# Attention steps moved between slots, routing spread over the tiles, and the first expert's weight splits placed later

## The chip, the core and the metric

The kernel runs on one core of a Trainium2 chip. A core has a matrix engine (TensorE, "PE"), a vector engine (VectorE, "DVE"), a scalar engine (ScalarE, "ACT"), GpSimd ("POOL") and SyncE ("SP"), which here only issues DMAs. Every engine takes its own instructions strictly in order and waits on semaphores for the others. The metric is the device time of one execution in microseconds (us).

## What is computed

4096 tokens of width 256 pass through three residual stages:

```python
x = x + 0.5 * ffn(layernorm(x))     # stage 1
x = x + attn(layernorm(x))          # attention in groups of 64 tokens, 16 heads of 16
x = x + 0.5 * ffn(layernorm(x))     # stage 2, the same weights
# ffn(x): shared = silu(x @ sg) * (x @ su) @ sd                  (256 -> 2048 -> 256)
#   routed: RMS norm, 8 router logits, top 2 of 8 experts, weights from a softmax;
#   each expert takes its first 640 tokens: silu(x @ rg[e]) * (x @ ru[e]) @ rd[e]   (256 -> 1024 -> 256)
# attn: q, k get an RMS norm times ln_w; causal softmax inside each group of 64 tokens
```

## The kernel before

Every fp32 product is made of three fp16 products: both operands are split into a high and a low half, and high x high, high x low, low x high are summed in PSUM (`TERMS`, L35).

The program has four phases. **Phase a**: front of stage 1 (layernorm, router, scatter) and the shared FFN of blocks 0 to 3 (a block is 512 tokens, four tiles of 128). **Phase b**: stage 1's eight experts. **Phase c**: the shared FFN of blocks 4 to 7 of stage 1 and then of blocks 0 to 6 of stage 2, with the attention of 32 tiles woven in. **Phase d**: stage 2's eight experts and the last shared block.

A shared block has 16 chunks (L406). A chunk is `gate_up` (L350): six matmuls of 512 columns into a gate bank and six into an up bank, out of three banks that rotate. In phase c ACT takes the tanh of the gate bank (L367), DVE multiplies it with the bank (`sl`, L368) and with the up bank (`sl`, L373), ACT casts the result to fp16 (`hh`, L375), and DVE takes the rest (`hl`, L376, two inputs in SBUF). The down product, twelve matmuls of 256 columns (L384), is held back until the next chunk's `gate_up` has been issued (`defer`, L97); its third matmul is the first that reads `hl`.

Attention and routing of a tile are a generator (`tile2`, L839) whose `yield`s are steps. `Tiles` (L730) starts a tile every `GAP_C` = 4 slots and takes one step of each live tile per slot; `drive` (L779) gives one slot per chunk. A tile's steps are: layernorm (`stats`, `two`), a transpose by DMA (`xt`), q, k, v (`pqk`, `pv`, L584 to L598), q and k norms and fp16 halves (`ss`, `qk`, `QK`, L602 to L620), transposes by DMA (`QT`, L624), scores (`psc`, `S`, L628 to L637), softmax (`amx`, `S` minus the maximum on POOL at L641, exp, `e16`, on POOL at L652), a transpose (`ET`, L655), the product with the values (`py`, `Y`), a transpose (`yt`, L681), projection (`pao`, `y`), and the front of stage 2 (`front_steps`, L697). POOL also forms `yp`, `X` and `xa` (all L172), the powers of -0.5 (L150, L592), parts of the routing weights (L245 to L266), and it issues the scatters: per tile four small copies (L339) and two indirect DMAs (L341).

The fourth tile of each block runs `route` (L239): the top two of eight for four tiles at once (L250 to L255), softmax weights on POOL, positions by small matmuls, then `scatters` (L310), one tile per step, tied behind an anchor instruction of POOL (L313).

In the experts (L466) each chunk's weights are loaded by SP, split by ACT (L105) and DVE (L106) into fp16 halves, and used; the chunk's buffers are two deep.

The order on each engine is not that of the source: a scheduler orders the instructions when the program is built. `issue_after` forces an instruction behind a named one on the same engine.

Of the kernel before, what the change touches and what calls it, by code (L numbers as in the profile page):

```python
# [20 lines left out]
P = 128  # L21
H = 256
# [3 lines left out]
WS = 16.0  # L26
XP = UP * WS
NB = 8
BT = 512
E = 8  # L30
# [7 lines left out]
class Net:  # L38
# [160 lines left out]
    @contextmanager  # L199
    def behind(self, on=True, *engines):  # L200

        with ExitStack() as st:
            if on:
                for k in engines:
                    st.enter_context(self.tc.issue_after(self.latest[k]))
            yield
# [18 lines left out]
    def logits(self, fb, t, xt):  # L225
# [11 lines left out]
        nc.scalar.copy(fb["L"][:, t], p)  # L237

    def route(self, R, b, fb, tiles):  # L239

        nc = self.nc
        sm = self.sm
        mv, rstd = fb["mv"], fb["rstd"]
        rs = sm.tile([P, 4], F32, name="rs")
# [3 lines left out]
        nc.gpsimd.tensor_tensor(out=rs, in0=rs, in1=self.mhalf[:, :4], op=ALU.pow)  # L248
        L = sm.tile([P, 4, E], F32, name="Ls")
        nc.vector.tensor_tensor(out=L, in0=fb["L"][:, :, 0], in1=fb["L"][:, :, 1], op=ALU.add)  # L250
        mx = sm.tile([P, 4, E], F32, name="mx")
        ix = sm.tile([P, 4, E], U32, name="ix")
        for t in range(4):
            nc.vector.max(out=mx[:, t, :], in_=L[:, t, :])
            nc.vector.max_index(out=ix[:, t, :], in_max=mx[:, t, :], in_values=L[:, t, :])  # L255
        dl = sm.tile([P, 4], F32, name="dl")
        nc.vector.tensor_tensor(out=dl, in0=mx[:, :, 1], in1=mx[:, :, 0], op=ALU.subtract)
        nc.gpsimd.tensor_tensor(out=dl, in0=dl, in1=rs, op=ALU.mult)
        nc.gpsimd.tensor_scalar_mul(dl, dl, 1.0 / WS)
        nc.gpsimd.tensor_tensor(out=dl, in0=self.e1, in1=dl, op=ALU.pow)  # L260
        w1 = sm.tile([P, 4], F32, name="w1")
        nc.gpsimd.tensor_scalar_add(w1, dl, 1.0)
        nc.gpsimd.tensor_tensor(out=w1, in0=w1, in1=self.mone, op=ALU.pow)
        nc.gpsimd.tensor_scalar_mul(w1, w1, 0.5 / WS)
        nc.gpsimd.tensor_tensor(out=dl, in0=dl, in1=w1, op=ALU.mult)
        nc.gpsimd.tensor_tensor(out=w1, in0=w1, in1=dl, op=ALU.subtract)  # L266
        ef = sm.tile([P, 4, 2], F32, name="ef")
        nc.vector.tensor_copy(ef, ix[:, :, 0:2])
        yield
        oh = sm.tile([P, 4, 2, E], F32, name="oh")  # L270
# [4 lines left out]
        nc.vector.tensor_tensor(out=M, in0=oh[:, :, 0, :], in1=oh[:, :, 1, :], op=ALU.add)  # L275
        yield
        pp = self.m1([P, 4, E], F32, "pp")
        nc.tensor.matmul(pp, lhsT=self.tri, rhs=M, start=True, stop=False)
# [11 lines left out]
        nc.vector.tensor_reduce(out=pos, in_=pk, axis=AX.X, op=ALU.add)  # L290
        yield
        df = sm.tile([P, 4, 2], F32, name="df")
        nc.vector.scalar_tensor_tensor(
# [10 lines left out]
        last = self.scatters(R, b, fb, di, w1, dl, ef, 1 if b == NB - 1 else tiles.apart)  # L304
        if b == NB - 1 or tiles.apart == 1:
            yield from last
        else:
            tiles.extra.append(last)

    def scatters(self, R, b, fb, di, w1, dl, ef, every):  # L310

        for t in range(4):
            with self.tc.issue_after(self.anchor.ins):  # L313
                self.scatter(R, b, fb, t, di, w1, dl, ef)
            for _ in range(every):
                yield
# [149 lines left out]
    def experts(self, R, rg, ru, rd, cur, also=iter(())):  # L466

        nc = self.nc
        for e in range(E):
            x, ids, wts = cur["x"], cur["id"], cur["w"]  # L470
# [3 lines left out]
            for c in range(8):  # L474
                if e == 0 and c < 2:
                    wc, wd = self.chunks[c]
                else:
                    r = self.raw.tile([P, 2, 2, P], F32, name="re", tag="raw")
                    for i, s in enumerate((rg, ru)):
                        nc.sync.dma_start(  # L480
                            out=r[:, i], in_=s[e, :, c * P:(c + 1) * P].rearrange("(k p) f -> p k f", p=P))
                    r2 = self.raw.tile([P, H], F32, name="re2", tag="raw2")
                    nc.sync.dma_start(out=r2, in_=rd[e, c * P:(c + 1) * P])
                    wc = self.raw.tile([P, 2, 2, 2, P], F16, name="wc")
                    self.split(wc[:, 0], wc[:, 1], r)
# [55 lines left out]
    def attn_init(self, ln_w):  # L541
# [15 lines left out]
        for i in range(2):  # L557
# [3 lines left out]
            self.V2.append(v)  # L561

    def attn_tile(self, R, j, x2, new_fb):

        nc = self.nc
# [33 lines left out]
        yield  # L599
        yield  # L600
# [5 lines left out]
        for i in range(2):  # L606
# [8 lines left out]
            else:  # L615
# [4 lines left out]
                    out=s[:, :, 1::2, :], in0=src, in1=s[:, :, 0::2, :], op=ALU.subtract)  # L620
        yield
        QT = a.tile([P, 2, 24, 64], F16, name="QT")
        for g in range(2):
            nc.sync.dma_start_transpose(  # L624
                out=QT[:, g], in_=self.QK[g * 64:(g + 1) * 64].rearrange("p j c -> p (j c)"))
        yield
        yield
        S = a.tile([P, 16, 64], F32, name="S")  # L628
        for g in range(2):
            p = self.m1([P, 8, 64], F32, "psc")  # L630
            for jj in range(8):
                nc.tensor.matmul(
                    p[:, jj, :], lhsT=QT[:, g, 2 * jj:2 * jj + 2, :].rearrange("p r q -> p (r q)"),
                    rhs=QT[:, g, 16 + jj, :], start=True, stop=True)
            nc.vector.tensor_tensor(  # L635
                out=S[:, g * 8:(g + 1) * 8, :], in0=p,
                in1=self.mask.unsqueeze(1).to_broadcast([P, 8, 64]), op=ALU.add)  # L637
        yield
        mx = self.sm.tile([P, 16], F32, name="amx")
        nc.vector.tensor_reduce(out=mx, in_=S, axis=AX.X, op=ALU.max)  # L640
        self.anchor = nc.gpsimd.tensor_tensor(  # L641
            out=S, in0=S, in1=mx.unsqueeze(2).to_broadcast([P, 16, 64]), op=ALU.subtract)
        for g in range(2):
            for d in range(2):
                nc.scalar.copy(  # L645
                    V2[d * 64:(d + 1) * 64, g, :, :, 0:32],
                    vs[g * 64:(g + 1) * 64].rearrange("p l (j c) -> p l j c", c=32))
        yield
# [5 lines left out]
        ET = a.tile([P, 16, P], F16, name="ET")  # L654
        nc.sync.dma_start_transpose(out=ET, in_=e16.rearrange("p h l k -> p (h l k)"))  # L655
        yield
        yield
        Y = a.tile([P, 2, 8, 16], F32, name="Y", tag="yy")
        for g in range(2):
# [7 lines left out]
            for r in range(2):  # L667
# [3 lines left out]
                    in1=rc[sl].unsqueeze(2).to_broadcast([64, 8, 16]), op=ALU.mult)  # L671
        yield
        y = self.tok.tile([P, H], F32, name="y")
# [6 lines left out]
        for r in range(2):  # L680
            nc.sync.dma_start_transpose(out=yt[:, r], in_=yp[r * 64:(r + 1) * 64])  # L681
        yield
        yield
# [115 lines left out]
def macaron(ctx, tc, x, w_qkv, ln_w, w_proj, router_w, rg, ru, rd, sg, su, sd, out):  # L799
# [20 lines left out]

    def tail(R, h, b, t):
        if t == 3:
            yield from n.route(R, b, fbs[(h, b)], tiles)
# [101 lines left out]
```

## Time and profile before

| what | value |
|---|---|
| median of 3 runs (lowest, highest) | 1809.57 us (1809.15, 1809.93) |
| profiled execution, device time | 1811.83 us |
| its span | 1809.8 us |
| busy PE, DVE, ACT, POOL | 1777.4, 1194.7, 949.8, 752.2 us |
| matmuls | 13652 |
| granted TensorE clock, mean | 0.999 |

The profiled execution took 2.3 us more than the median of the timed ones, and 2.0 us of it lie outside the span. A busy PE counts every matmul from its start to its modelled end, and the ends overlap the next starts, so stalls shorter than about 0.16 us don't show as idle time.

### The profile page before, as it was taken

The numbers are of one execution on the slowest core, as the hardware profiler recorded it, in microseconds if no ns is written. First come the engines' busy times: TensorE is split into PE (matmuls) and PEld (weight loads), VectorE is DVE, ScalarE is ACT, GpSimd is POOL, SyncE is SP. The second block draws the span as 40 slices with busy tenths as digits, with TensorE's granted clock in tenths as the row PEclk, the third lists the DMA queues.
The fourth block names the chain that finished last, engine by engine and source line by source line (L and its number), as shares of the span: only waits on it lengthen the run. The fifth ranks groups of instructions, "written<-read, shape, count | busy, mean of one in ns | idle before, by whom it ended". The sixth has DMA issues, their size and how long they took to land.

```text
span 1809.8 us, 37358 instructions
## 1 busy us (share of the span) xinstructions
PE 1777.4 (98%) x13652; PEld 1200.8 (66%) x13652; DVE 1194.7 (66%) x2905; ACT 949.8 (52%) x2053; POOL 752.2 (42%) x1072
## 2 busy tenths in 40 slices
PE   9999999999999999999999999999999999999998
PEld 5666657777777556665666666566555677777765
DVE  7766636666665678877777778778655566666643
ACT  5433334555554456666666666656333355555542
POOL 3676711211112445576767777675430011122210
PEclk9999999999999999999999999999999999999999
DMA  7333133555543356767677675756212045455420
GB/s 222 105 102 116 38 69 88 120 118 120 115 112 66 70 101 101 133 119 138 125 130 144 114 147 108 143 100 125 56 22 71 18 109 115 111 119 121 100 47 13
DMA packets 437545, 185.16 MB, mean 102 GB/s; under 512 B 302193, under 2 KB 434733, under 8 KB 437360
## 3 DMA queue, kind: packets, MB, share of 16 engines
q1 hardware_dynamic: 418880, 160.81, 40.7%
q0 software_dynamic: 17664, 21.17, 6.9%
q8 instruction: 107, 1.75, 0.4%
q10 hardware_dynamic: 816, 0.79, 0.1%
q14 instruction: 78, 0.64, 0.1%
HBM read 78.16 MB, written 42.21 MB: 67 GB/s over the span
## 4 chain that ended last, share of the span: by engine, by line
PE 65%; DVE 9%; issue 9%; POOL 8%; ACT 5%; DMA 2%; SPq 1%; POOLq 0%; DVEq 0%; ACTq 0%
PE pgu L360 42%; PE po L384 21%; POOL xg L341 2%; DVE sl L368 2%; DVE hl L376 2%; POOL S L641 1%; DVE amx L640 1%; DVE S L635 1%; DVE sl L373 1%; ACT sl L367 1%; POOL e L652 1%; ACT V L645 1%; POOL X L339 1%; POOL ss L592 1%; DMA y<-acc 1%
## 5 line engine op out<-in xcount | busy, mean ns | idle before, releaser
L360 PE MATMUL pgu<-xb,sgu 128*128 128x512 f16 x3072 | 736.1, 379 | 10.3 <-DVE sl L368 5.6
L375 ACT CAST hh<-sl 128x512 f16<-128x512 f32 (+2 forms) x512 | 272.9, 533 | 538.1 <-DVE sl L373 513.2
L360 PE MATMUL pgu<-xe,wc 128*128 128x384 f16 (+1 forms) x3072 | 497.6, 299 | 0.0
L360 PEld LDWEIGHTS <-sgu 128*128 128x128 f16 x3072 | 292.8, 98 | 282.8 <-issue 15.2
L373 DVE SCALAR_TENSOR_TENSOR sl<-pgu,sl 128x512 f32<-128x512 f32 (+2 forms) x512 | 301.1, 588 | 265.0 <-PE pgu L360 230.8
L376 DVE TENSOR_TENSOR hl<-sl,hh 128x512 f16<-128x512 f32 (+2 forms) x512 | 316.4, 618 | 152.4 <-ACT hh L375 139.3
L384 PEld LDWEIGHTS <-hh 128*128 128x128 f16 x3328 | 321.3, 98 | 106.8 <-ACT hh L375 3.9
L360 PEld LDWEIGHTS <-wc 128*128 128x128 f16 x3072 | 300.6, 98 | 91.8
L384 PE MATMUL po<-sdw,hh 128*128 128x256 f16 x2048 | 349.7, 272 | 2.5 <-ACT hh L375 2.2
L384 PE MATMUL po<-sdw,hl 128*128 128x256 f16 x1024 | 249.1, 273 | 10.0 <-DVE hl L376 9.8
L384 PE MATMUL po<-wd,hh 128*128 128x256 f16 x1280 | 222.5, 273 | 0.0
L506 POOL DMA_INDIRECT out_dram<-eo,eidscatter x40 | 64.3, 1607 | 342.4 <-DVE eo L505 308.7
L371 ACT ACTIVATE sl<-pgu 128x384 f32<-128x384 f32 (+1 forms) x336 | 159.0, 473 | 75.7 <-PE pgu L360 48.5
L384 PEld LDWEIGHTS <-hl 128*128 128x128 f16 x1664 | 162.7, 98 | 51.3 <-DVE hl L376 16.8
L506 POOL DMA_INDIRECT acc<-eo,eidscatter x40 | 64.9, 1621 | 293.4 <-DVE eo L505 259.4
L368 DVE SCALAR_TENSOR_TENSOR sl<-sl,pgu 128x512 f32<-128x512 f32 x176 | 120.1, 682 | 54.9 <-ACT sl L367 52.3
L341 POOL DMA_INDIRECT xg<-X,di x128 | 133.4, 1042 | 45.6 <-issue 23.0
L384 PE MATMUL po<-wd,hl 128*128 128x256 f16 x640 | 148.2, 273 | 0.0
L367 ACT ACTIVATE sl<-pgu 128x512 f32<-128x512 f32 x176 | 104.3, 593 | 29.2 <-PE pgu L360 28.2
L105 ACT ACTIVATE wc<-re 128x512 f16<-128x512 f32 x124 | 78.1, 630 | 73.4 <-PE pgu L360 59.3
L106 DVE SCALAR_TENSOR_TENSOR wc<-re,wc 128x512 f16<-128x512 f32 x124 | 85.6, 690 | 25.0 <-ACT wc L105 19.1
L641 POOL TENSOR_TENSOR S<-S,amx 128x1024 f32<-128x1024 f32 x32 | 63.6, 1988 | 70.4 <-DVE amx L640 70.0
(159 smaller groups left out, 1730.7 us busy)
## 6 DMA issues: line engine op xcount, KB each, us to landing
re<-in_L_ffn_rg_dram SPq DMA_DIRECT2D x124, 128.0 KB
re<-in_L_ffn_ru_dram SPq DMA_DIRECT2D x124, 128.0 KB
re<-in_L_ffn_rd_dram SPq DMA_DIRECT2D x124, 128.0 KB
y<-acc SPq DMA_DIRECT2D x64, 128.0 KB
y<-in_L_attn_x_dram SPq DMA_DIRECT2D x32, 128.0 KB
acc<-xr SPq DMA_DIRECT2D x16, 256.0 KB
out_dram<-xr SPq DMA_DIRECT2D x16, 256.0 KB
x<-y SPq DMA_DIRECT2D x28, 128.0 KB
```

What stands on the lines that cost most here:

```text
L106: nc.vector.scalar_tensor_tensor(out=lo, in0=src, scalar=WS, in1=hi, op0=ALU.mult, op1=ALU.subtract)
L341: i = nc.gpsimd.indirect_dma_start(out=R["xg"][:, :], out_offset=bass.IndirectOffsetOnAxis(ap=di[:, t, k:k + 1], axis=0), in_=X, in_offset ...
L360: nc.tensor.matmul(p, lhsT=wc[:, w, i, k, :], rhs=x[:, 2 * a + k, :], start=(j == 0), stop=(j == 5))
L367: nc.scalar.activation(s, p, AF.Tanh, scale=0.5 / XP)
L368: nc.vector.scalar_tensor_tensor(out=s, in0=s, scalar=1.0, in1=p, op0=ALU.add, op1=ALU.mult)
L371: self.latest[0] = nc.scalar.activation(s, p, AF.Silu, scale=1.0 / XP).ins
L373: self.latest[1] = nc.vector.scalar_tensor_tensor(out=s, in0=ps[1], scalar=1.0 / XP / (2.0 * XP if tanh else 1.0), in1=s, op0=ALU.mult, op ...
L375: nc.scalar.copy(h[0], s)
L376: nc.vector.tensor_tensor(out=h[1], in0=s, in1=h[0], op=ALU.subtract)
L384: nc.tensor.matmul(o, lhsT=h[a][:, t * P:(t + 1) * P], rhs=wd[:, w], start=(c == 0 and j == 0 and t % 2 == 0), stop=(c == nch - 1 and j == 2),
L506: i = nc.gpsimd.indirect_dma_start(out=R["acc"][:, :], out_offset=bass.IndirectOffsetOnAxis(ap=ids[:, t:t + 1], axis=0), in_=eo, in_offset ...
L641: self.anchor = nc.gpsimd.tensor_tensor(out=S, in0=S, in1=mx.unsqueeze(2).to_broadcast([P, 16, 64]), op=ALU.subtract)
```

## The change

Line numbers of the changed file are not used below; the operations keep the names and lines of the kernel before.

1. **Attention's steps.** One `yield` fewer between q, k, v and the q/k norms; one more before `QT`, one more after it (three slots from the `QT` transposes to the scores instead of two), one more after `ET`, none between `Y` and `yp`, one more after `yt`. The copies of the values into `V2` (L645), four in one step, become two in the scores' step and two in the next. `vs` has two buffers. The tiles' slot counter starts at -2.
2. **Routing.** The top two of eight are found tile by tile (`top2`). `route` is cut at other places: the POOL chain for `rs` first, the exponential and its companions two steps later, `w1` and what follows one step after that.
3. **Scatters.** In phase c one tile is scattered every four slots, after three empty slots, as an extra generator; before, the four tiles of a block were scattered in four successive slots. The pool of `X` has 8 buffers instead of 6. Two more POOL powers (L150 in `front_steps`, L592) become anchors for scatters.
4. **Experts.** The splits of expert 0's chunks 2 to 7 are forced, on ACT and DVE, behind the last silu and `sl` of the chunk two before.

```diff
+    def top2(self, fb, t):
+        nc = self.nc
+        if t == 0:
+            fb["mx"] = self.sm.tile([P, 4, E], F32, name="mx")
+            fb["ix"] = self.sm.tile([P, 4, E], U32, name="ix")
+        L = self.sm.tile([P, E], F32, name="Ls")
+        nc.vector.tensor_tensor(out=L, in0=fb["L"][:, t, 0], in1=fb["L"][:, t, 1], op=ALU.add)
+        nc.vector.max(out=fb["mx"][:, t, :], in_=L)
+        nc.vector.max_index(out=fb["ix"][:, t, :], in_max=fb["mx"][:, t, :], in_values=L)
...
     def scatters(self, R, b, fb, di, w1, dl, ef, every):
+        for _ in range(3 if every == 4 else 0):
+            yield
         for t in range(4):
...
+        marks = []
...
-                    self.split(wc[:, 0], wc[:, 1], r)
                     wd = self.raw.tile([P, 2, H], F16, name="wd")
-                    self.split(wd[:, 0], wd[:, 1], r2)
+                    with self.behind(e == 0, 0, 1, mark=marks[-2]):
+                        self.split(wc[:, 0], wc[:, 1], r)
+                        self.split(wd[:, 0], wd[:, 1], r2)
...
+                marks.append(list(self.latest))
...
+    def values(self, V2, vs, g):
+        for d in range(2):
+            self.nc.scalar.copy(
+                V2[d * 64:(d + 1) * 64, g, :, :, 0:32],
+                vs[g * 64:(g + 1) * 64].rearrange("p l (j c) -> p l j c", c=32))
...
-        nc.gpsimd.tensor_tensor(out=ss, in0=ss, in1=self.mhalf[:, :2], op=ALU.pow)
+        self.anchor = nc.gpsimd.tensor_tensor(out=ss, in0=ss, in1=self.mhalf[:, :2], op=ALU.pow)
...
-        vs = a.tile([P, 2, H], F16, name="vs")
+        vs = a.tile([P, 2, H], F16, name="vs", bufs=2)
...
         yield
-        yield
         for i in range(2):
...
         yield
+        yield
         QT = a.tile([P, 2, 24, 64], F16, name="QT")
...
+        yield
         yield
         yield
         S = a.tile([P, 16, 64], F32, name="S")
...
-        self.stats(y, fb["mv"][:, t, :], fb["rstd"][:, t:t + 1], keep is None)
+        self.stats(y, fb["mv"][:, t, :], fb["rstd"][:, t:t + 1], True)
...
-    with n.phase("c", BT, 2, 6, SLC):
+    with n.phase("c", BT, 2, 8, SLC):
         n.attn_init(ln_w)
-        tiles = Tiles(tile2, 32, GAP_C, 1)
+        tiles = Tiles(tile2, 32, GAP_C, GAP_C)
+        tiles.slot = -2
```

The order in which the changed program's instructions stand was compared with the order before. PE has the same 13652 matmuls. In phase c the order before differs from tile to tile: one tile in four carries the scatters, one the top two of eight, two others the POOL chains. In the changed order the four tiles of a block are nearly alike. On POOL a tile reads

```
S (L641), X, xa (L172), 4 copies (L339), 2 scatters (L341), e (L652), yp (L172), ss (L592), QK (L613 x2, L619), rstd, arstd (L150)
```

from the 9th or 10th tile to the 29th, with the `rs` chain at the end of one tile in four and the chain for `dl` and `w1` ahead of `rstd` in the next. On DVE four chunks of a tile read

```
mv amv ve ve S S hl nm nm amx sl368 sl373 | sl368 hl sl373 | rc rc Y hl ss sl368 qk qk vs Ls sl373 | mx ix hl sl368 y st st sl373
```

On ACT the four copies into `V2` still stand together in most tiles, behind exp and `e`, and ahead of a chunk's `hh`.

More of the change, by code (lines that the diff above doesn't have):

```diff
@@ L199, in behind @@
     @contextmanager
-    def behind(self, on=True, *engines):
+    def behind(self, on=True, *engines, mark=None):
         with ExitStack() as st:
@@ L204, in behind @@
                 for k in engines:
-                    st.enter_context(self.tc.issue_after(self.latest[k]))
+                    st.enter_context(self.tc.issue_after((mark or self.latest)[k]))
             yield
@@ L242, in route @@
         sm = self.sm
-        mv, rstd = fb["mv"], fb["rstd"]
+        mv, rstd, mx, ix = fb["mv"], fb["rstd"], fb["mx"], fb["ix"]
         rs = sm.tile([P, 4], F32, name="rs")
@@ L248, in route @@
         nc.gpsimd.tensor_tensor(out=rs, in0=rs, in1=self.mhalf[:, :4], op=ALU.pow)
[L249 to L255, printed above, removed]
+        yield
         dl = sm.tile([P, 4], F32, name="dl")
         nc.vector.tensor_tensor(out=dl, in0=mx[:, :, 1], in1=mx[:, :, 0], op=ALU.subtract)
[L258 to L266, printed above, removed]
         ef = sm.tile([P, 4, 2], F32, name="ef")
         nc.vector.tensor_copy(ef, ix[:, :, 0:2])
-        yield
         oh = sm.tile([P, 4, 2, E], F32, name="oh")
@@ L276, in route @@
         yield
+        nc.gpsimd.tensor_tensor(out=dl, in0=dl, in1=rs, op=ALU.mult)
+        nc.gpsimd.tensor_scalar_mul(dl, dl, 1.0 / WS)
+        nc.gpsimd.tensor_tensor(out=dl, in0=self.e1, in1=dl, op=ALU.pow)
         pp = self.m1([P, 4, E], F32, "pp")
@@ L291, in route @@
         yield
+        w1 = sm.tile([P, 4], F32, name="w1")
+        nc.gpsimd.tensor_scalar_add(w1, dl, 1.0)
+        nc.gpsimd.tensor_tensor(out=w1, in0=w1, in1=self.mone, op=ALU.pow)
+        nc.gpsimd.tensor_scalar_mul(w1, w1, 0.5 / WS)
+        nc.gpsimd.tensor_tensor(out=dl, in0=dl, in1=w1, op=ALU.mult)
+        nc.gpsimd.tensor_tensor(out=w1, in0=w1, in1=dl, op=ALU.subtract)
         df = sm.tile([P, 4, 2], F32, name="df")
@@ L304, in route @@
         last = self.scatters(R, b, fb, di, w1, dl, ef, 1 if b == NB - 1 else tiles.apart)
-        if b == NB - 1 or tiles.apart == 1:
+        if b == NB - 1:
             yield from last
@@ L598, in attn_tile @@
             out=vs[:, 1, :], in0=pv, scalar=1.0 / XP, in1=vs[:, 0, :], op0=ALU.mult, op1=ALU.subtract)
-        yield
         yield
@@ L625, in attn_tile @@
                 out=QT[:, g], in_=self.QK[g * 64:(g + 1) * 64].rearrange("p j c -> p (j c)"))
+        yield
         yield
@@ L637, in attn_tile @@
                 in1=self.mask.unsqueeze(1).to_broadcast([P, 8, 64]), op=ALU.add)
+        self.values(V2, vs, 0)
         yield
@@ L642, in attn_tile @@
             out=S, in0=S, in1=mx.unsqueeze(2).to_broadcast([P, 16, 64]), op=ALU.subtract)
[L643 to L647, printed above, removed]
+        self.values(V2, vs, 1)
         yield
@@ L655, in attn_tile @@
         nc.sync.dma_start_transpose(out=ET, in_=e16.rearrange("p h l k -> p (h l k)"))
+        yield
         yield
@@ L671, in attn_tile @@
                     in1=rc[sl].unsqueeze(2).to_broadcast([64, 8, 16]), op=ALU.mult)
-        yield
         y = self.tok.tile([P, H], F32, name="y")
@@ L681, in attn_tile @@
             nc.sync.dma_start_transpose(out=yt[:, r], in_=yp[r * 64:(r + 1) * 64])
+        yield
         yield
@@ L821, in tail @@
     def tail(R, h, b, t):
+        n.top2(fbs[(h, b)], t)
         if t == 3:
```

## The prediction

> **What bounds the kernel now.** I read the page first, then PE's waits in the stretch where attention is woven in, then busy times by stage, then single instructions.
>
> ```profile
> PE 1777.4 (98%) x13652; PEld 1200.8 (66%) x13652; DVE 1194.7 (66%) x2905; ACT 949.8 (52%) x2053; POOL 752.2 (42%) x1072
> ```
>
> The waits of PE from 720 to 1280 us (total, times, longest):
>
> ```profile
> PE po L384 <- DVE hl L376: 8.5, 13, 0.7
> PE pgu L360 <- DVE sl L368: 5.2, 6, 0.9
> ```
>
> Busy times by stage (window, length, then busy us and count of PE, PEld, DVE, ACT, POOL, the granted clock, DMA share, GB/s):
>
> ```profile
> 800.00:1240.00 440.00, 426.49 (x3606) 268.75 (x3603) 338.44 (x871) 283.83 (x600) 312.07 (x429) 1.00 0.68 130
> 1240.00:1300.00 60.00, 57.85 (x475) 36.30 (x473) 41.72 (x107) 27.49 (x55) 34.64 (x55) 0.97 0.33 61
> 1300.00:1345.00 45.00, 45.00 (x293) 27.36 (x291) 28.57 (x70) 14.90 (x27) 13.06 (x34) 1.00 0.12 33
> ```
>
> PE is the bound at the full clock, so only its stalls can be won. In attention's stretch its waits are for DVE. Idle time understates them: taken from the starts of successive matmuls, against 0.216 us for 512 columns and 0.109 for 256, PE loses 18.1 us in 800 to 1240, 5.7 in 587 to 800, 4.5 in 1240 to 1300, nothing in 1300 to 1345. Attention's stage thus holds 28 us, the two entries into the experts another 4.6; the rest of the span next to nothing.
>
> ```profile
> 969.57 1.93 POOL S L641
> ...
> 1051.05 1.93 POOL S L641
> ```
>
> In the chain of waits (start, us, what) the pattern returns every 81.5 us, a block of four tiles: 20.4 per tile. Pure PE work of a tile's four chunks is 19.6 (four times 2.59 + 1.31, from the chain's runs of twelve matmuls, and 4.0 of attention). So 0.8 per tile is stalled.
>
> **Part 4, the experts' splits.** On ACT before:
>
> ```profile
> 251.08 0.63 ACT L105 ACTIVATE wc<-re 128x512 f16<-128x512 f32 x1 [6.65 <-DMA re<-in_L_ffn_rg_dram]
> 251.62 0.60 ACT L375 CAST hh<-sl 128x512 f16<-128x512 f32 x1
> ...
> 252.28 0.61 PE L384 MATMUL po<-sdw,hh 128*128 128x256 f16 x4 [1.66 <-ACT hh L375]
> ```
>
> A split that waits for its weights stands ahead of the shared block's `hh`, and PE waits. At 1363 it is the same (idle 1.73 and 0.24). From start to start the losses are 2.2 and 2.4. Afterwards the splits stand behind chunk 0's silu; two chunks of some 5 us each remain until chunk 2 needs them, and a split takes 1.0 on ACT and 1.1 on DVE. I count 4.3 gained.
>
> **Parts 1 to 3, a gain first.** Following the new order, DVE no longer has a tile with the top two, the exponent, the residual and the scores together; every local stall of before has slack on PE's side. If no queue were longer than PE's 19.6, nearly all 28 us would go.
>
> **The cost.** Two scatters and four copies now stand in every tile of POOL, between `S` and `e`, and `ss`, without which DVE cannot do `qk`, stands behind them. This closes a loop through DVE and POOL, which I add up by differences of starts:
> - DVE, from a tile's last `sl` (L373) to `amx`: four small ones 0.3, `S` twice 1.2, `hl` 0.6, `nm` twice 0.25, `amx` 1.21, less 0.08 of overlap: 3.5 (starts of 512-column instructions in a row lie 0.60 apart though each takes 0.68).
> - POOL: hop 0.13, `S` 1.90, `X` and `xa` 1.24, copies and scatters 3.0 (row pair below: 966.46 to 969.57 is 3.1), `e` 2.13, `yp` 0.62, `ss` 0.7: 9.7.
> - DVE: `qk` twice and `vs` 1.15, `Ls` 0.1, `sl` 0.68, ACT's `hh` with hops 0.73, `hl` 0.6, `sl` 0.6, `y` 0.33, `st` 0.66, `sl` 0.68: 5.6 with the first hop.
>
> Sum 18.8, below 19.6: no stall.
>
> ```profile
> 966.46 0.17 POOL L339 COPY X<-tokid 128x1 f32<-128x1 f32 x1
> ...
> 967.14 1.01 POOL L341 DMA_INDIRECT xg<-X,di  x1 [0.16 <-POOL X L339]
> 968.46 1.09 POOL L341 DMA_INDIRECT xg<-X,di  x1 [0.30 <-issue]
> 969.57 1.92 POOL L641 TENSOR_TENSOR S<-S,amx 128x1024 f32<-128x1024 f32 x1
> ...
> 687.17 2.13 POOL L652 TENSOR_TENSOR e<-S,e 128x1024 f16<-128x1024 f32 x1 [2.24 <-ACT e L651]
> ...
> 687.65 2.20 DVE L376 TENSOR_TENSOR hl<-sl,hh 128x512 f16<-128x512 f32 x1 [1.40 <-ACT hh L375]
> ```
>
> The last two rows change this. `hl` usually takes 0.69; here it takes 2.20, ending 0.55 after `e`. The Trainium skill (SBUF — State Buffer, "Who interferes with whom") says that a DVE instruction with two SBUF inputs and a GpSimd instruction that reads SBUF exclude each other for their whole length, whichever starts first. Row and rule agree that it blocks; the rule adds that it must happen at every overlap and in both directions. It speaks against this change, because three of the loop's `hl` now fall on long POOL work: one becomes ready 0.1 before POOL's `S` ends (costs POOL 0.43), one while `e` runs, since its `hh` stands on ACT behind exp, `e16` and four `V2` copies (0.50), one while the last `QK` runs (0.64). Counted from the end of `amx`: POOL's `S` runs to 2.0, and `sl368`, `sl373`, `hh` make the first `hl` ready at 1.9; `e` runs from 6.75 to 8.9, while exp (to 3.15), `e16` (4.2), the copies (6.6) and `hh` (7.2) make the second ready at 7.3; with the delays `ss` ends at 10.65, the last `QK` runs from 12.95 to 14.1, and the third is ready at 13.35. With the rule the loop is 20.3, without it 18.8. I take 20.3: the second and third overlaps hold by 0.4 or more, and in place of the first `hl` would meet `X`.
>
> So each of the 21 tiles with scatters costs 20.3 - 19.6 = 0.7, together 15. Two POOL chains lie in the loop too: `rs` (about 2.3) ends some 0.85 after `amx`, the chain of `dl` and `w1` (4.3) delays `rstd` by about 0.4, and `M`, `n` cost DVE 0.25: 1.5 per block, five times 7.5. Less 2 of slack before the loop first binds: 21 us of stalls, where those tiles had 18.5. These are worked out from rows; their ends are 0 (locks missed) and 34 (0.6 more per tile).
>
> **The rest.** Tiles 0 to 8 have no scatters, so a loop of under 19.6: I take 3.5 of stalls for 5.7. The gap at 1285 to 1294, 4.4 us with the clock at half for 3.4, stood beside six scatters in a row that are now spread; whether they cause it the trace can't say. I count half, 2. Three more small DVE instructions per tile (0.15 each) run while `hl` waits for `hh`. The `V2` copies and the second `vs` cost no work; PE's cover for them is that chunk's 1.8 us before `hl` is needed. The extra slots lengthen a tile by some six slots: the last routing stands about 19 chunks before the end of phase c, instead of 23, and 4 scatter slots fit. SP's queue keeps its ten issues per tile (some 12 us of 19.6); `QT` gets a slot more, so it lands earlier than needed. Eight `X` buffers cover the 23 slots that an `X` lives.
>
> Sum: -4.3 + 2.5 - 2.2 - 2 = -6 us. The profiled execution's span of 1809.8 would become 1804. I take off the same from the median, 1809.6 to 1803.6; the 2.3 between profiled and timed stays out.
>
> **Rivals.**
> - *The locks are missed*, the loop is 18.8 and PE bound: 21 us of stalls shrink to 2, so 1785. For it: a regular order, and in before most `hl` took 0.69. Against: the starts above.
> - *The loop is longer still (slower).* If `hl` goes ahead of `e` and the scatters take what they did from 953.24 to 956.93, 3.7 instead of 3.1, POOL's chain grows by 0.6 in 21 tiles: +13, so 1816. It ends slower than before once the loop passes 20.6, beyond the tie by 0.2% from about 20.8.
> - *A wait for a DMA takes over*, as `ET`, `yt` and `QT` share SP with the store of `y`: 0.5 per tile over 32 tiles is +16, so 1820. Against: each landing has over a slot to spare.
> - That the steps don't move is excluded by the order of the built program.
>
> **Chances.** The forecast 0.50, spread 1797 to 1811; locks missed 0.17; longer loop 0.27; DMA 0.06. A measurement of this kernel tells about 0.2%, 3.6 us. Faster: 0.33 of the forecast's and all of the second, 0.50. Slower: nearly all of the last two and a little of the first, 0.34. The rest 0.16. The range leaves out half of the fast case and the ends of the slow ones.
>
> **What would show it.** Right: waits of PE for `hl` twice per tile, evenly, period 20.4 to 20.7 per tile; `hl` of 1.3 to 2.2 us beside `e` and `QK`; no wait for `hh` at either entry into the experts. Wrong: periods of 19.6 and no waits (locks missed), or POOL's `S` more than 21 us apart; or PE waiting for a transpose.

## The result and the profile after

The changed kernel takes **1815.78 us** (median of 7 runs, 1815.11 to 1816.61), the one before 1809.36 us beside it (7 runs, 1808.24 to 1811.58). The ratio is **1.0034** (95% interval 1.0023 to 1.0044): slower by some 6 us. The profiled execution took 1816.61 us, its span 1814.8, so 5.0 more than the span before.

The page's line of busy times:

```profile
PE 1781.6 (98%) x13652; PEld 1197.6 (66%) x13652; DVE 1265.6 (70%) x2953; ACT 955.1 (53%) x2053; POOL 768.6 (42%) x1072
```

DVE is busy 71 us longer than before. It has 48 instructions more, but most of this isn't work: an instruction that is held while one of POOL's runs counts as busy. From 800 to 1240 us the `hl` alone are lengthened by 49 us in all, against 6 before. PE's waits from 720 to 1280 us (total, times, longest):

```profile
PE po L389 <- DVE hl L381: 16.5, 36, 0.8
PE pl L230 <- DMA xb<-X: 0.5, 1, 0.5
```

The waits for `sl` are gone, those for `hl` have doubled. (L381 is L376 of the kernel before; from here on lines are those of the changed file: `sl` L373 and L378, `hh` L380, `S` on POOL L658, `e` L665, `ss` L607, copies and scatters L344 and L346.) Busy times by stage, columns as in the prediction:

```profile
800.00:1240.00 440.00, 423.65 (x3527) 260.48 (x3526) 392.54 (x878) 281.49 (x595) 312.98 (x418) 1.00 0.64 127
1240.00:1300.00 60.00, 57.47 (x498) 36.34 (x497) 49.53 (x111) 32.74 (x65) 37.52 (x49) 1.00 0.51 92
```

In attention's stage DVE is busy 392.5 us in place of 338.4, and in the same 440 us PE gets through fewer matmuls (3527 against 3606). In the prediction's own measure, starts of successive matmuls less 0.216 or 0.109 us each, PE's lost time by stretch is:

| stretch, us | what is there | before | after | difference | forecast |
|---|---|---|---|---|---|
| 205-275 and 1345-1400 | entries into the experts | 5.16 | 0.00 | -5.2 | -4.3 |
| 587-800 | entry into attention, tiles 0 to 8 | 5.63 | 8.58 | +3.0 | -2.2 |
| 800-1240 | tiles 9 to 29 | 18.01 | 25.75 | +7.7 | +2.5 |
| 1240-1300 | last tiles, scatters | 4.52 | 3.26 | -1.3 | -2 |
| elsewhere | start, phases a and b, the end | 7.1 | 7.8 | +0.7 | 0 |
| sum | all | 40.4 | 45.4 | +5.0 | -6 |

A stall of 0.55 us that ends at 587.45 before and at 585.42 after is counted under "elsewhere" in both. But for rounding, the sum of the differences is the difference of the spans, so nothing is missing. The splits and the last tiles came out near the forecast; the two terms of attention's phase did not.

Now one tile of the steady state, in the timeline of POOL (start, length, instruction, in brackets the idle time before it and what ended it):

```profile
1044.20 1.90 POOL L658 TENSOR_TENSOR S<-S,amx 128x1024 f32<-128x1024 f32 x1 [1.54 <-DVE amx L657]
1046.06 0.68 POOL L172 TENSOR_TENSOR X<-z,X 128x256 f16<-128x256 f32 x1
1046.69 0.68 POOL L172 TENSOR_TENSOR xa<-z,xa 128x256 f16<-128x256 f32 x1
1047.31 0.65 POOL L344 COPY X<-tokid 128x1 f32<-128x1 f32 x1
...
1050.01 0.98 POOL L346 DMA_INDIRECT xg<-X,di  x1 [0.31 <-issue]
1051.01 2.14 POOL L665 TENSOR_TENSOR e<-S,e 128x1024 f16<-128x1024 f32 x1
1053.09 1.14 POOL L172 TENSOR_TENSOR yp<-Y,yp 128x256 f16<-128x256 f32 x1
1054.34 0.73 POOL L607 TENSOR_TENSOR ss<-ss,mhalf 128x2 f32<-128x2 f32 x1
...
1064.92 1.90 POOL L658 TENSOR_TENSOR S<-S,amx 128x1024 f32<-128x1024 f32 x1 [2.14 <-DVE amx L657]
```

and what DVE does meanwhile:

```profile
1046.90 1.01 DVE L381 TENSOR_TENSOR hl<-sl,hh 128x512 f16<-128x512 f32 x1
...
1050.50 3.21 DVE L381 TENSOR_TENSOR hl<-sl,hh 128x512 f16<-128x512 f32 x1
...
1058.08 0.98 DVE L381 TENSOR_TENSOR hl<-sl,hh 128x512 f16<-128x512 f32 x1 [0.34 <-ACT hh L380]
...
1063.57 1.21 DVE L657 TENSOR_REDUCE amx<-S 128x16 f32<-128x1024 f32 x1
```

From `S` to `S` 20.72 us pass, where the prediction's loop has 20.3. From `S` to the end of `ss` POOL waits for nothing but its own issue (twice 0.3); from there DVE is at work, with small gaps, until `amx`. `hl` without company takes 0.68; here it takes 1.01, 3.21 and 0.98, and the first small copy on POOL 0.65 where the others take 0.17. These are the locks, two or three per tile, near where they were forecast. The row of 3.21 occurs in one tile of four; in the others `hl` begins some 0.4 after `e` and takes 2.3. A block of four tiles takes 83.7 us (81.6 before), since the chain of `dl` makes one tile in four 0.7 to 0.9 longer.

The second thing stands at the entry into attention's phase, in the timeline of the changed kernel:

```profile
597.55 2.66 POOL L564 MEMSET QK<- 128x3072 f16 x1 [2.29 <-PE pgu L365]
...
600.25 0.24 POOL L559 TENSOR_SCALAR_AFFINE_SELECT mask<-mask 128x64 f32<-128x64 f32 x1
...
600.53 0.19 DVE L562 COPY mask<-m 64x64 f32<-64x64 f32 x1 [7.04 <-POOL mask L559]
600.75 0.69 DVE L378 SCALAR_TENSOR_TENSOR sl<-pgu,sl 128x512 f32<-128x512 f32 x1
...
601.50 1.72 PE L365 MATMUL pgu<-xb,sgu 128*128 128x512 f16 x6 [2.92 <-DVE sl L378]
```

A copy that builds the causal mask stands on DVE ahead of a shared chunk's `sl`. It waits for POOL's `affine_select`, which stands behind the memset of `QK` (2.7 us). PE waits 2.92 and then runs at a granted clock of 0.50 to 0.52 from 603 to 606, which makes 4.75 us lost in 587 to 612 in place of 0.94. So the gain at the first entry into the experts is given back here.

In the kernel before PE waits only 0.78 at this place. The memset of `QK` in before, and in e1, which is before with part 4 alone:

```profile
596.85 3.23 POOL L555 MEMSET QK<- 128x3072 f16 x1
```

```profile
592.47 3.24 POOL L559 MEMSET QK<- 128x3072 f16 x1
```

There it begins at once behind the mask's first memset. In the changed kernel it waits 2.29 us for a PE product first, and this is what makes the mask late. That PE comes earlier, since part 4 saves it 2.7 us, isn't the cause: in e1 the whole set-up comes 4.4 us earlier with it, and PE waits 0.67. Every run with parts 2 and 3, whole or for the most part, that leaves the set-up as it is has this wait of 2.1 to 2.3 us, also with attention's steps as before (f3), and none without those parts has it (e1, e8, f4). A larger pool of `X` shifts the memory of what is placed behind it, so `QK` may now lie where PE still reads; that wasn't tried.

### The profile page after: what moved, and what is told of

It is laid out like the page before. It is cut to its first block, busy times and chain, and to the rows that moved or that the text cites. A ratio compares the mean times of both kernels' runs of the same rounds, so it can differ in the third digit from the quotient of the medians.

```text
span 1814.8 us, 37381 instructions
## 1 busy us (share of the span) xinstructions
PE 1781.6 (98%) x13652; PEld 1197.6 (66%) x13652; DVE 1265.6 (70%) x2953; ACT 955.1 (53%) x2053; POOL 768.6 (42%) x1072
## 4 chain that ended last, share of the span: by engine, by line
PE 34%; DVE 12%; POOL 11%; issue 6%; ACT 3%; DMA 1%; POOLq 0%; DVEq 0%; ACTq 0%; SPq 0%
PE pgu L365 22%; PE po L389 11%; POOL e L665 2%; DVE sl L378 2%; DVE hl L381 2%; POOL xg L346 2%; DVE S L651 1%; DVE sl L373 1%; DVE amx L657 1%; POOL yp L172 1%; POOL xa L172 1%; ACT hh L380 1%; POOL ss L607 1%; DVE st L145 1%; POOL S L658 1%
## 5 line engine op out<-in xcount | busy, mean ns | idle before, releaser
L380 ACT CAST hh<-sl 128x512 f16<-128x512 f32 (+2 forms) x512 | 273.0, 534 | 530.8 <-DVE sl L378 525.2
L378 DVE SCALAR_TENSOR_TENSOR sl<-pgu,sl 128x512 f32<-128x512 f32 (+2 forms) x512 | 301.0, 588 | 264.0 <-PE pgu L365 232.9
L381 DVE TENSOR_TENSOR hl<-sl,hh 128x512 f16<-128x512 f32 (+2 forms) x512 | 355.3, 694 | 175.0 <-ACT hh L380 173.0
L376 ACT ACTIVATE sl<-pgu 128x384 f32<-128x384 f32 (+1 forms) x336 | 159.1, 474 | 76.2 <-PE pgu L365 47.9
L346 POOL DMA_INDIRECT xg<-X,di x128 | 135.1, 1055 | 45.1 <-issue 30.4
L373 DVE SCALAR_TENSOR_TENSOR sl<-sl,pgu 128x512 f32<-128x512 f32 x176 | 119.7, 680 | 28.9 <-ACT sl L372 27.9
L150 POOL TENSOR_TENSOR rstd<-ve,mhalf 128x1 f32<-128x1 f32 x64 | 41.2, 645 | 117.5 <-DVE ve L148 117.1
```

What stands on the lines that cost most here:

```text
L346: i = nc.gpsimd.indirect_dma_start(out=R["xg"][:, :], out_offset=bass.IndirectOffsetOnAxis(ap=di[:, t, k:k + 1], axis=0), in_=X, in_offset ...
L373: nc.vector.scalar_tensor_tensor(out=s, in0=s, scalar=1.0, in1=p, op0=ALU.add, op1=ALU.mult)
L376: self.latest[0] = nc.scalar.activation(s, p, AF.Silu, scale=1.0 / XP).ins
L378: self.latest[1] = nc.vector.scalar_tensor_tensor(out=s, in0=ps[1], scalar=1.0 / XP / (2.0 * XP if tanh else 1.0), in1=s, op0=ALU.mult, op ...
L380: nc.scalar.copy(h[0], s)
L381: nc.vector.tensor_tensor(out=h[1], in0=s, in1=h[0], op=ALU.subtract)
```

## Experiments

Each median stands beside runs of the kernel before on the same chip, 1809.4 to 1811.9 us from one chip to the next; so compare ratios. "Block" is the time of four tiles, from the starts of POOL's `S` over four blocks; "lost" is PE's lost time in 800 to 1240. The kernels in which part of the computation is other are named at their place.

| run | made from | median us | ratio (95%) | block | lost |
|---|---|---|---|---|---|
| before | | 1809.4 | 1 | 81.6 | 18.0 |
| after | | 1815.8 | 1.0034 (1.0023-1.0044) | 83.7 | 25.8 |
| e1 | before + part 4 | 1804.0 | 0.9954 (0.9941-0.9968) | 81.6 | 17.8 |
| e2 | after, mask first | 1812.3 | 1.0003 (0.9994-1.0011) | 83.6 | 25.7 |
| e3 | after, scatters a slot earlier | 1809.8 | 0.9990 (0.9980-0.9999) | 82.4 | 20.8 |
| e4 | after, `hl` with one input | 1796.8 | 0.9917 (0.9901-0.9933) | 79.8 | 9.6 |
| e5 | after, top 2 for four tiles at once | 1811.6 | 1.0012 (1.0006-1.0019) | 83.6 | 25.2 |
| e6 | after, scatters in a burst | 1813.5 | 1.0020 (1.0012-1.0029) | 83.4 | 25.8 |
| e7 | after, `sl` in PSUM | 1814.1 | 1.0023 (1.0013-1.0032) | 81.8 | 21.5 |
| e8 | before + part 4, `sl` in PSUM | 1788.2 | 0.9883 (0.9868-0.9898) | 79.3 | 5.5 |
| f3 | after, steps as before | 1794.7 | 0.9912 (0.9895-0.9929) | 79.6 | 6.2 |
| f4 | before + new steps | 1818.0 | 1.0044 (1.0028-1.0061) | 82.9 | 24.2 |
| i1 | after, one more after `e` | 1827.9 | 1.0102 (1.0085-1.0119) | 85.5 | 35.1 |
| i2 | after, one more after `QK` | 1814.7 | 1.0026 (1.0017-1.0036) | 83.7 | 25.6 |
| g1 | f3, mask first | 1791.9 | 0.9898 (0.9882-0.9915) | 79.7 | 6.2 |
| g2 | g1, `sl` in PSUM | 1788.8 | 0.9881 (0.9865-0.9898) | 78.7 | 1.1 |

**e1, part 4 alone.** The kernel before with the diff's `marks` and nothing else.

> The kernel before with part 4 of the change alone. My theory: the two entries into the experts lose their waits (2.7 us of lost PE time at 205 to 275, 2.5 at 1345 to 1400, both gone in the changed kernel), and nothing gives it back: 1809.4 - 5 = 1804.4. Rival: the 2.7 us won at the first entry is waited for again at the entry of attention's stage, where DVE holds PE until the mask is there: 1807.

Lost time in the two entries is 0.02, and at the entry into attention PE waits no longer than before, so the rival falls. This part is as forecast, and alone makes the kernel faster: by the ratio 8 us, of which 5 lie at the two entries and 1.7 in 1240 to 1300.

**e2, the entry.** After, with

```diff
-        for m, base in ((self.mask, 0), (m2, -64)):
+        for m, base in ((m2, -64), (self.mask, 0)):
...
-        nc.gpsimd.memset(self.QK, 0.0)
+        with self.tc.issue_after(i.ins):
+            nc.gpsimd.memset(self.QK, 0.0)
```

where `i` is the last `affine_select`.

> The changed kernel with the clearing of QK forced behind the mask's select on POOL. My theory: the stall of 3.1 us at 601 us, with the half clock behind it (2.4 us), is the price of a mask that stands behind a clearing of QK which waits for PE: 1815.8 - 4.5 = 1811.3, and no half clock there. Rival: PE is held by attention's other first work (loads of y after the last scatter-add), so the wait only moves: 1815.

Lost time in 587 to 612 falls from 4.75 to 1.83 and the clock there is full (1.00). That the stall comes from the mask behind the memset is shown: 3 us.

**e3, e5, e6: where the scatters and the top two stand.** e3 has two empty slots ahead of a block's scatters in place of three. e5 takes the top two of four tiles at once, in the fourth tile. e6 scatters in a burst, as before. In this order:

```diff
-        for _ in range(3 if every == 4 else 0):
+        for _ in range(2 if every == 4 else 0):
```

```diff
+        if t < 3:
+            return
+        L = self.sm.tile([P, 4, E], F32, name="Ls")
+        nc.vector.tensor_tensor(out=L, in0=fb["L"][:, :, 0], in1=fb["L"][:, :, 1], op=ALU.add)
+        for i in range(4):
+            nc.vector.max(out=fb["mx"][:, i, :], in_=L[:, i, :])
...
```

```diff
-        if b == NB - 1:
+        if b == NB - 1 or tiles.apart == 1:
...
-        tiles = Tiles(tile2, 32, GAP_C, GAP_C)
+        tiles = Tiles(tile2, 32, GAP_C, 1)
```

> The changed kernel with two empty slots ahead of the scatters instead of three; on POOL this puts the copies and the two scatters of a tile behind ss instead of between S and e. Loop theory: the chain from S to ss falls by 3.1 us, the loop by about 2.5 to 18.3, below PE's 19.6: tile periods of 19.6 to 19.9 instead of 20.9, 20 us less: 1795. Rival (the new order of attention's steps on DVE is what makes hl late, wherever the scatters stand): periods stay near 20.8 and the time between 1812 and 1816.

> The changed kernel with the top two of eight taken for four tiles at once again; POOL's order stays that of the changed kernel. Theory: Ls (two SBUF inputs, 0.56 us instead of the 0.1 I counted) and the max pair lie on the loop in every tile; three tiles in four lose them: periods of those tiles fall by 0.2 to 0.5, 4 to 8 us less than the changed kernel: 1809. Rival: they run while hl waits for POOL's QK anyway, and cost nothing: 1815, periods unchanged.

> The changed kernel with the scatters of a block in successive slots again, as before (part 3 undone, parts 1, 2 and 4 kept). Loop theory: two tiles of each block are without scatters and fall to PE's 19.6 to 19.9, one has one scatter tile outside S to ss, one has two scatter tiles between S and e and grows by about 3 us: a block of 82 to 83 instead of 83.6, 3 to 9 us less than the changed kernel. Rival (part 3 is what carries the change): a block grows beyond 84, slower than the changed kernel.

All three missed. In e3 the scatters and the chain of `dl` fall together, and two of four tiles grow to 21.9 and 22.2 while the others shrink; DVE's order changed too. e5 leaves the steady state as it was: `Ls` and its companions cost nothing there, and only 720 to 800 gains (2.85 to 0.99). e6 says most. Its tiles take 21.4, 20.3, 20.8 and 20.7: two without scatters win 0.4 and 0.6, and one with the burst loses 0.7 again. Scatters and copies take 3.2 of a tile's POOL time in after, so a tile without them should have won far more. Measured from the end of `amx`, `ss` ends after 9.3 in place of 10.95, and why not earlier is seen on ACT, in e6's timeline:

```profile
1003.34 1.06 ACT L662 ACTIVATE S<-S 128x1024 f32<-128x1024 f32 x1
1004.43 1.05 ACT L664 CAST e<-S 128x1024 f16<-128x1024 f32 x1
1005.38 2.50 ACT L574 COPY V<-vs 64x512 f16<-64x512 f16 x4
1007.90 0.62 ACT L380 CAST hh<-sl 128x512 f16<-128x512 f32 x1
1008.43 0.40 ACT L171 CAST yp<-Y 128x256 f16<-128x256 f32 x1
```

There is no idle time between these rows: exp, `e16` and the four copies stand ahead of `hh` and `yp`, and POOL's `yp` and `ss` wait for ACT. Beside POOL's branch from `S` to `ss` lies one through ACT, only 1.7 us shorter. Taking the scatters out of POOL can win no more than that; so they alone are not what makes the loop long. PE loses as much as in after, though the `hl` are lengthened by only 9 us in all in place of 49.

**e4, the lock.** After, with `hl` made by a reduction of `sl` alone, one input in SBUF. The low half is then a copy of `sl` and not the rest that `hh` leaves, so the output differs there.

```diff
-        nc.vector.tensor_tensor(out=h[1], in0=s, in1=h[0], op=ALU.subtract)
+            nc.vector.tensor_reduce(out=h[1], in_=s.unsqueeze(2), axis=AX.X, op=ALU.add)
```

> The changed kernel with hl formed by an instruction with one SBUF input (hl becomes sl, not sl minus hh, so the low part of the product is not the reference's). Lock theory: no hl takes more than 0.75 us, the loop is 18.8 to 19.2, PE bounds: periods of 19.6 to 19.9, 1795. Rival (POOL's chain alone sets the period, locks cost little): periods of 20.5 or more, 1812 to 1815. The scheduler also moves some hl, so a mixed result would be read from the durations.

No `hl` takes over 0.69, a block takes 79.8 and PE loses 9.6. From the end of `amx` to the end of `ss` it is 10.24 on the mean in place of 10.97. But this `hl` reads only `sl`: it no longer waits for ACT's `hh` either, so the edit takes away the branch through ACT together with the lock. The scheduler also moved some `hl` ahead of one or two neighbours on DVE. How much of the gain is the lock, e4 can't say.

**e7 and e8, the lock taken away with the right values.** `sl` is written back into its PSUM bank, so `hl` has one SBUF input; e7 does it in after, e8 in e1.

```diff
-            out=s, in0=ps[1], scalar=1.0 / XP / (2.0 * XP if tanh else 1.0), in1=s, op0=ALU.mult, op1=ALU.mult).ins
-        nc.scalar.copy(h[0], s)
-        nc.vector.tensor_tensor(out=h[1], in0=s, in1=h[0], op=ALU.subtract)
+            out=ps[1], in0=ps[1], scalar=1.0 / XP / (2.0 * XP if tanh else 1.0), in1=s, op0=ALU.mult, op1=ALU.mult).ins
+        nc.scalar.copy(h[0], ps[1])
+        nc.vector.tensor_tensor(out=h[1], in0=ps[1], in1=h[0], op=ALU.subtract)
```

> The changed kernel with the gated product sl (L373) written back into its PSUM bank; hh and hl read it there, so hl has one SBUF input. Lock theory: no hl over 0.75 us, periods of 19.6 to 20, as in the run with one input: 1797. Rival: the bank is held until hl is done and PE waits for banks instead: a wait of PE's gate products for hl appears and the time stays above 1808.

> The kernel before with part 4 and with sl in PSUM. Before, 11 of 86 hl between 800 and 1240 us were over 0.9 us, 6 us of blocking in all, against 51 of 85 and 49 us after the change. Lock theory: little to win here, at most the 6 us: 1799 to 1804. Rival (the bank in PSUM helps by itself, whatever the locks): as large a gain as in the changed kernel, some 19 us: 1786.

e7 missed: the locks are gone, but a block falls only from 83.7 to 81.8. The scheduler put `X` and `xa` late on POOL in some tiles, and PE now waits for a DMA. The rival's sign, a wait of `pgu` for `hl`, isn't there either. PE's waits in e7 from 720 to 1280:

```profile
PE pl L230 <- DMA xb<-X: 9.4, 6, 2.0
PE po L389 <- DVE hl L381: 8.4, 8, 1.4
```

e8 stands 0.7% below e1, 13 us, more than the theory allowed and nearer to what the rival said (1786): in the kernel before, `hl` was blocked only 6 us in all from 800 to 1240. What the other part is, POOL's own delays or the other order, wasn't separated.

**f1 and f2, the copies moved.** In f1 (after) and f2 (e6) the four copies into `V2` stand one slot after `QK`.

```diff
         yield
+        self.values(V2, vs, 0)
+        self.values(V2, vs, 1)
         yield
         QT = a.tile([P, 2, 24, 64], F16, name="QT")
...
-        self.values(V2, vs, 0)
...
-        self.values(V2, vs, 1)
```

> After, with the four V2 copies of a tile taken out of the scores' step and put one slot after QK, where ACT is idle; POOL's order stays as in after. In after exp, e16 and the four copies (1.1 + 1.0 + 2.5) stand on ACT ahead of the second hh, so a branch through ACT runs beside POOL's branch (S, X, xa, scatter, e) and is only some 0.5 us a tile shorter. Theory (two branches of nearly one length, tied by the lock): hh comes 2.5 us sooner, hl is done before e starts, its lock with e goes, POOL's own branch remains: 83.5 us per block fall to 80.5 to 82, stalls from 800 to 1240 from 25.8 to 15 to 20, time 1806 to 1811. Rival (the scatters and copies on POOL alone set the loop): periods stay within 0.2 of after, time 1814 to 1816.

> The same move of the V2 copies, in the kernel whose scatters go in a burst as before. Theory of two branches: now both are shorter, the two tiles of a block without scatters fall from 20.3 to 20.8 to at most 19.7, and only the tiles with the chain of dl and with the burst stay long; stalls from 800 to 1240 fall from 25.8 to 8 to 14, time 1797 to 1804. Rival (neither branch, but the order of the steps on DVE sets the period): tiles stay at 20.3 and more, time 1811 to 1815.

1837.2 (ratio 1.0147, 1.0130 to 1.0164) and 1823.7 (1.0075, 1.0058 to 1.0092): both missed, and they decide nothing. With a tile every four slots the copies now stand ahead of the product `Y` of the tile two before, which reads the same of two buffers, so that product is taken with other values; and the scheduler set the copies ahead of the casts of `QK` and gave DVE another order. Whether ACT's branch can be shortened stays open.

**f3 and f4, part 1 undone and alone.** f3 is after with the `attn_tile` of before; f4 is before with the `attn_tile` and `values` of after.

> After, with attention's steps in the slots of before; a scatter tile per four slots, the top two per tile and the splits stay. Theory (the steps' new order sets the longer period): tiles return to 17.7 to 20, the long tile of 25.4 is gone because the scatters are spread, a block takes 79 to 81 us, time 1796 to 1804. Rival (the spread scatters set it): 83 us and more per block, time 1812 to 1818.

> Before, with the attention steps' new slots alone; scatters in a burst, routing and splits as before. Theory (the new order sets the longer period, through hh behind exp, e16 and the copies on ACT): 83 us and more per block, stalls from 800 to 1240 of 24 to 27 us, time 1815 to 1821. Rival (the scatters spread over the tiles are what makes after longer): 81.5 or less per block, time 1803 to 1810.

Both near what the theory has: 79.6 and 82.9 per block. The waits in f3 from 720 to 1280, and then in f4:

```profile
PE po L389 <- DVE hl L381: 4.1, 6, 0.7
```

```profile
PE po L384 <- DVE hl L376: 8.4, 19, 0.8
PE pl L230 <- DMA xb<-X: 5.7, 6, 1.3
PE pgu L360 <- DVE sl L368: 3.0, 6, 0.6
```

PE's wait in f4 from 205 to 275, at the first entry into the experts:

```profile
PE po L384 <- ACT hh L375: 4.1, 1, 4.1
```

The rest of the change, without the new steps, wins 16 us, of which part 4 alone has 8. The new steps alone cost 8, but not all of it in attention: 5.5 us are lost at the two entries into the experts (10.7 in place of 5.2), where no attention runs and a split on ACT waits longer for its weights. In attention's phase, 587 to 1300, they cost 2: 6 more in 800 to 1240, 4 less around it. The two parts also hang together. With the old steps, spreading the scatters and the routing shortens a block from 81.6 to 79.6 (e1, f3); with the new steps it takes 82.9 to 83.7, spread or not (f4, e6, after). The long tile of before (25.4) is gone in f3, whose tiles take 18.6 to 21.0.

**i1 and i2, one instruction inside and beside the loop.** The same small power on POOL in every tile of after, once behind `e`, once behind the last `QK`.

```diff
+        with self.tc.issue_after(self.anchor.ins):
+            du = self.sm.tile([P, 2], F32, name="du")
+            nc.gpsimd.tensor_tensor(out=du, in0=self.e1[:, 0:2], in1=self.mhalf[:, :2], op=ALU.pow)
```

> After, with one more POOL instruction of 128x2 in every attention tile (as ss, 0.7 us), right after e and ahead of yp and ss. Theory (the loop amx, S, scatter, e, ss, DVE, amx sets the period): every tile of the steady state is longer by its whole length, 83.5 us per block become 86.1 to 86.6, and over some 22 tiles the time grows by 13 to 17, to 1829 to 1833. Rival (something beside this loop sets the period, and POOL has room after e): 83.5 to 84.2 per block, time 1815 to 1819.

> The same extra instruction, placed after the last QK of the tile, where POOL waits 3.2 us for DVE. Theory: it lies beside the loop, only the one tile of a block with the chain of dl can grow, by up to 0.7; 83.5 to 84.2 per block, time 1815 to 1819. Rival (POOL's sheer load sets the period): as i1, 86 and more per block, 1829 to 1833.

POOL in i1, and then in i2:

```profile
1012.62 2.14 POOL L665 TENSOR_TENSOR e<-S,e 128x1024 f16<-128x1024 f32 x1
1014.71 1.21 POOL L668 TENSOR_TENSOR du<-e,mhalf 128x2 f32<-128x2 f32 x1
1015.90 0.66 POOL L172 TENSOR_TENSOR yp<-Y,yp 128x256 f16<-128x256 f32 x1
```

```profile
1057.94 1.14 POOL L637 TENSOR_TENSOR du<-e,mhalf 128x2 f32<-128x2 f32 x1
1061.19 0.55 POOL L150 TENSOR_TENSOR rstd<-ve,mhalf 128x1 f32<-128x1 f32 x1 [2.11 <-DVE ve L148]
```

Behind `e`, the instruction lengthens the loop: from `amx` to the end of `ss` 11.51 in place of 10.97, a block 85.5 in place of 83.7, the time by 12 us. Behind `QK` it takes 1.14 and costs nothing; POOL has room there. So the loop sets the period, and POOL's load does not. The size was overestimated: POOL's part grows by 0.54 per tile and the period by 0.45, not 0.7, because in most tiles `du` (1.21) now waits for the lock that `yp` waited for, and `yp` takes 0.66 in place of 1.14.

**g1 and g2, what beats both.** g1 is f3 with e2's edit, g2 is g1 with e7's.

> f3 (steps as before, the rest of the change kept) with the causal mask's second half made first and the memset of QK behind it. Theory: the PE stall at the entry, 4.9 in 587 to 612 in f3, falls to about 2 and the half clock behind it goes; steady state as f3; time 1790 to 1793. Rival (the entry is late for another reason): 1794 to 1796.

> g1 with the scaled gate product left in PSUM, so that hl has one SBUF input. Theory (what is left of the stalls in 800 to 1240, 6.2 in f3, is the lock): they fall to 1 to 3, time 1785 to 1789. Rival (the other order of instructions that this brings costs as in e7): 1793 or more.

g1 came as expected, lost time in 587 to 612 down from 4.90 to 1.92. g2 loses 1.1 in 800 to 1240, but 7.6 in 612 to 720 (5.2 in g1), where PE waits 2.9 for three transposes and 2.0 for `hh`. It is level with the simpler e8: ratios 0.9881 and 0.9883. Both are 1.2% faster than the kernel before.

## Why the prediction was wrong

**The splits** were right: 4.3 forecast, 5.2 measured, and e1 shows it alone.

**The loop** through DVE and POOL is there: i1 against i2 shows that it sets the period. Its parts, measured in the plain tiles from the end of one `amx` to the next:

| part of the loop | forecast | after |
|---|---|---|
| POOL to the end of `ss`, with the first two locks | 10.6 | 10.95 |
| from there DVE to the end of `amx`, with the third | 9.7 | 9.71 |
| period of a plain tile | 20.3 | 20.7 |
| chains of `dl` and `rs`, per block | 1.5 | 1.0 |
| block | 82.7 | 83.7 |

Two steps failed. The first is the size of POOL's term in the loop, 10.6 forecast and 10.95 measured. From the first copy to the start of `e` it is 3.70, of which 0.48 is the lock, so copies and scatters take 3.2 and not 3.0; the first lock is 0.05 dearer, and 0.1 passes between `yp` and `ss`. A third of a microsecond looks small. But the loop lies above PE's 19.6, so every tenth of it costs PE a tenth in each of 21 tiles: 1.0 per block in 5.25 blocks is about the 4.75 us between 21 of lost time forecast and 25.75 measured. That turns the sum from -6 to about -1; the tiles ahead of it turn the sign. The prediction had put the point from which the loop is slower than before at 20.6, and its own forecast at 20.3 with one decimal of precision. The time lies outside the spread of its likeliest case, 1797 to 1811.

**What makes the loop long** it had only in part. It took the scatters and copies on POOL for the cause, and a tile without them to be under 19.6. The tiles of e6 without scatters take 20.3 and 20.8, and f4's block, with the scatters in a burst, 82.9: a second branch, through ACT, is nearly as long. So the new order of the steps makes the longer period, and that 20.3 came so near to 20.7 is in part luck.

The three locks fell near where they were computed, with one exchange: the first `hl` met `xa` or the first small copy instead of `S`. The rule weighed there (the Trainium skill, SBUF — State Buffer, "Who interferes with whom") agrees with the rows, and without the locks the sum, 18.8, would have given no stall at all. But the locks aren't what the longer period needs: in f4 and e6 the `hl` are lengthened by 9 us each in place of 49, and their blocks take 82.9 and 83.4. What the locks cost in the changed kernel stays open: e7, which takes them away and keeps `hl` behind `hh`, has 81.8 with a new wait for a DMA, and e4 takes away a branch with them.

**Tiles 0 to 8** are the second step that failed: forecast to win 2.2, they lost 3.0. The set-up of attention's phase was put at nothing, in the timeline and in the sum. Its memset came to wait for PE, which costs 3 us by e2. Behind it 612 to 720 won 2.8, and 720 to 800 lost 1.9; e5 shows that the per-tile top two are the cause there.

**The gap at 1285 to 1294** is gone, as half believed, but tiles 29 to 31 have new stalls in its place: -1.3 for -2. The burst of scatters alone doesn't make such a gap: e6 issues six scatters in a row from 1305 to 1314, and PE loses nothing in 1300 to 1345. What made it stays open.

**The rivals.** "The loop is longer still" gave 1816, and the time is 1815.8. It is right in kind and in part in detail: the scatters do take 3.2 to 3.7, but an `hl` that begins 0.5 ahead of `e` is held all the same. That its number fits is partly luck: of the 13 us it adds for the loop, the loop gave 5, and the entry into attention the rest. "The locks are missed" falls with the trace. "A wait for a DMA takes over" falls too: one wait of 0.5 us.

Why the old order is better is shown only as far as sums go. In f3 POOL's part from `amx` to `ss` is longer, 14.1 on the mean in place of 11.0, but the rest is 5.8 in place of 9.9: `hl`, `y`, `st` and `nm` run on DVE while POOL does `e`, scatters and `rstd`, and after `ss` only `qk`, `sl` and `S` stand before the next `amx`. With the new steps these stand in series: POOL's long part, then all of DVE's. That this overlap is the whole of the difference is argued from the rows, not tried.

## What to carry to other kernels

When a loop through two in-order engines comes within a few per cent of the bound, its length has to be summed to a tenth of a microsecond before the sign of a change can be told; test it with one small instruction put inside it and one beside it. Where steps are reordered, ask which part of each engine's work now stands in series with the other's, not how much work each has. And look at a phase's set-up too: which of its instructions stands in the queue of the engine that is needed next, and what that one waits for.

## What the runs showed of the hardware

- An `hl` that by its record had run 0.51 of its 0.68 us when `e` began on POOL was held until 0.56 after `e`'s end (the row of 3.21 us above; five times in the trace), while `e` took its usual 2.14. So the instruction whose record starts first is not safe. In before, against `xa`, both lost about 0.44 (1.11 in place of 0.69 and 0.67).
- POOL's issue of an indirect DMA doesn't block: the 101 `hl` of f3 that run beside nothing else of POOL's take at most 0.69, with two SBUF inputs.
- The lock hits small instructions too: `Ls`, 128x8, takes 0.56 to 0.57 beside `QK` in most tiles and 2.53 beside `e` in e6 (0.16 alone), and a POOL copy of 128x1 takes 0.65 in place of 0.17 beside `hl`.
